# Edge-attention scores with two halves' tiles together, one ring of six PSUM banks, and a written order on three engines

## The chip, the core and the metric

The kernel runs on one core of a Trainium2 chip. A core has TensorE (PE: matrix products and transposes, written into PSUM banks of 128 x 512 float32), VectorE (DVE), ScalarE (ACT), GpSimd (POOL) and SyncE (SP, which only issues DMAs). Each engine works through its own instructions in the order in which they were laid down, and waits on semaphores for the others. The metric is the device time of one execution in microseconds (us). In the profile, PEld is the loading of weights into TensorE, which overlaps PE, and SPq, ACTq and POOLq are the engines' instruction queues where they issue DMAs.

## The reference, cut to what matters

Four graph layers follow each other on x, 128 graphs of 64 nodes with 256 features. Each adds its output to x and normalises. The change lies in the third (layer 2), an attention over 512 edges with 4 heads of 64 features:

```python
Xq = (H @ W_lin.T).reshape(bt, n, h, dh)
Xv = (H @ W_val.T).reshape(bt, n, h, dh)
Qs = Xq[:, src]
Kt = Xq[:, dst]
e = jnp.einsum('behd,hd->beh', jax.nn.leaky_relu(Qs + Kt, 0.2), a)
e = e + jnp.log(A0[src, dst] + EPS)[None, :, None]
e_t = e.transpose(1, 0, 2)
m = jax.ops.segment_max(e_t, src, num_segments=n)
ex = jnp.exp(e_t - m[src])
attn = ex / jax.ops.segment_sum(ex, src, num_segments=n)[src]
Vt = Xv[:, dst].transpose(1, 0, 2, 3)
Y = jax.ops.segment_sum(attn[..., None] * Vt, src, num_segments=n)
return Y.transpose(1, 0, 2, 3).reshape(bt, n, d) @ W_out.T
...
x = _layernorm(x + layer(x))          # after each of the four layers
```

## The kernel before

**Data.** X lies in SBUF as 64 tiles of 128 rows (two graphs each) by 256 features. `NT` is 64, `NQ` and `HU` are 16. Layer 0 and most of layer 1 come first and are not touched.

**The last pass of layer 1** (`last_pass`) finishes layer 1 for two tiles at a time: `normed` scales them on ACT (L2039), PE transposes them (L2048), DVE adds them to X (`ln.add`: the join, L1350), takes statistics (L1353, L1354), and `flush` gets a factor by a chain of small instructions between DVE and ACT (`inv_sqrt`, L1272 to L1278, then L1365) and scales X on ACT (L1369). It is a generator that is driven beside the first 16 steps of layer 2.

**Scores** (`scores`) goes through 32 steps k of two tiles.
- `transposed(k)` transposes X on PE (L2136) and copies it to xT on DVE (L2138), two steps ahead.
- `maps(k + 1, xT)` multiplies xT by both weight matrices on PE (L2148). The query half w is split in a high part xh, copied on ACT into the reduced float32 type that the PE multiplies faster (L2153), and a remainder xl, a subtraction on DVE (L2154). The value half xv is copied on ACT (L2165) and sent to DRAM by SP (L2166).
- `edges(c)`, for each feature half c, multiplies xl and xh by a 0/1 matrix of the edges (L2188), which gives Q[src] + K[dst] of 512 edges for 128 features in one bank. ACT copies the bank to SBUF as xs (L2194), DVE makes the leaky relu in place (L2195): 4 tiles a half, 8 a step.
- `products` multiplies xs by the vector a (the table az) into score banks sc (L2124): 8 matmuls a half, each into 32 rows.

The order of a step is: edges of half 0, maps, edges of half 1, then both halves' products; in the first 16 steps the last pass stands between these and the products are issued a half at a time. Beyond that a scheduler settles the order of each engine; `after` makes the products of a cluster wait together.

**PSUM.** The stage uses eight banks: `pp` has two (tag "m": transposes, maps, mixing, W_out), `pg` two pairs (tag "l": edge tiles), `pc` two (tag "sc": scores).

**Softmax and values.** After 16 steps the scores of half of the graphs are complete. `softmax` adds log A, subtracts the segment maximum by two scans (DVE: L2231, L2235, L2236), exponentiates (ACT), transposes and sums by matmuls, and scatters the result to DRAM by indirect DMAs on POOL (L2275); `fetch` reads it back as a table M on SP and POOL (L2285). Then `values` runs beside the last scoring steps and beside layer 3: `mapped` loads xv back as xr on POOL's queue (L2300), `load` copies a piece mc of the table on ACT (L2292), `mixed` multiplies on PE (L2312) and copies yT on ACT (L2315), and W_out (L2335) is followed by `ln.add`, which flushes every four tiles.

**Layer 3** starts as values go on; its POOL addition is L2404.

The driver reads, cut:

```python
run(*beside * 4)                    # last_pass alone
run(*[sc_] * (NQ - 1))              # scoring steps, last_pass inside
soft += [softmax(h) for h in range(2)]
run(*[sc_] * (HU - NQ + 1))
run(*[sc_, soft[0]] * 6)
fetch(0)
run(*[sc_] * 3)
constants()
run(*[sc_, val] * 7)
```

Of the kernel before, what the change touches and what calls it, by code (L numbers as in the profile page):

```python
# [8 lines left out]
F32 = mybir.dt.float32  # L9
# [7 lines left out]
N = 64  # L17
NB = 128
D = 256
# [1317 lines left out]
class Norm:  # L1337
# [6 lines left out]
    def add(self, t, src, n=1, dve=0):  # L1344

        nc = self.nc
        if not self.todo:
            self.mv = self.pool.tile([P, self.n, 2], F32, tag="ln_mv", name="ln_mv")
        x = self.X[:, t : t + n, :].rearrange("p n d -> p (n d)")
        nc.vector.tensor_tensor(x, src, x, ALU.add)  # L1350
        for k in range(t, t + n):
            st = self.pool.tile([P, 6], F32, tag="ln_st", name="ln_st")
            nc.vector.bn_stats(st, self.X[:, k, :])  # L1353
            nc.vector.bn_aggr(self.mv[:, len(self.todo), :], st)  # L1354
            self.todo.append(k)
        if len(self.todo) == self.n:
            self.flush(dve)

    def flush(self, dve=0):
        nc, n = self.nc, len(self.todo)  # L1360
        rs = self.pool.tile([P, self.n], F32, tag="ln_rs", name="ln_rs")
        inv_sqrt(nc, self.pool, rs[:, :n], self.mv[:, :n, 1], 1e-5)
        if self.act:
            sh = self.pool.tile([P, self.n], F32, tag="ln_sh", name="ln_sh")
            nc.vector.scalar_tensor_tensor(sh[:, :n], self.mv[:, :n, 0], -1.0, rs[:, :n], ALU.mult, ALU.mult)  # L1365
        for k, t in enumerate(self.todo):
            x = self.X[:, t, :]
            if self.act and k < n - dve:
                nc.scalar.activation(x, x, AF.Identity, bias=sh[:, k : k + 1], scale=rs[:, k : k + 1])  # L1369
                continue  # L1370
            nc.vector.tensor_scalar(x, x, self.mv[:, k, 0:1], rs[:, k : k + 1], ALU.subtract, ALU.mult)
        self.todo = []


@with_exitstack
def tile_adj_resnorm(ctx: ExitStack, tc: tile.TileContext, I: dict, out: bass.AP, layers: int = 4):
# [655 lines left out]
    def last_pass():  # L2032

        ln = Norm(nc, sy, X, 8, act=True)

        def normed(h):
            y = sy.tile([P, 2, 2 * P], F32, tag="y", name="y")
            for c in range(2):
                s.activation(y[:, c, :], Y[h // 2][:, c, h % 2 * 2 * P : (h % 2 + 1) * 2 * P], AF.Identity,  # L2039
                             bias=sh2[:, c : c + 1], scale=sc2[:, c : c + 1])  # L2040
            return y

        y = normed(0)
        for h in range(2 * NQ):
            ps = pp.tile([P, 512], F32, tag="m", name="m")
            for i in range(2):
                for c in range(2):
                    te.transpose(ps[:, i * D + c * P : i * D + (c + 1) * P], y[:, c, i * P : (i + 1) * P], ident)  # L2048
            with in_order(v, h < 3):
                ln.add(2 * h, ps, 2)  # L2050
            if h == 1:
                keep_awake(pg.tile([P, 2, 512], F32, tag="l", name="l")[:, 0, :], 2)
            yield
            with in_order(s, h < 5):
                if h < 2 * NQ - 1:
                    y = normed(h + 1)
            with in_order(s, h < 5), in_order(v, h < 3):
                if h < 3 or h % 2 == 0 or h == 2 * NQ - 1:
                    ln.flush()
            yield  # L2060
# [10 lines left out]
    with ExitStack() as l2:  # L2071
# [3 lines left out]
        pp = own1(l2, name="l2p", bufs=2, space=PSUM)  # L2075
        sx = own1(scoring, name="l2x", bufs=2, side="right")
        pg = own1(scoring, name="l2g", bufs=2, space=PSUM)
# [17 lines left out]
        for c in range(2):  # L2095
            for h in range(2):
                o = (h + 1) * HU - 1
                v.tensor_tensor(az[:, c, o : o + 1], heads[:, h : h + 1], acol[:, c : c + 1], ALU.mult)
# [5 lines left out]
        taken, drawn, last = {}, {}, []  # L2104
        beside = [iter(())]
        soft = []

        def after(ins, those, how=mybir.DependencyClass.Sync):
            for i in those:
                tc.add_manual_dep(ins.ins, i.ins.name, mybir.DependencyInfo(how, mybir.DependencyReason.DATA),  # L2110
                                  reason="together")

        def products(todo, held):

            xss = [held.pop(x) for x in todo]
            mms = []
            for (k, c), (xs, _) in zip(todo, xss):
                half, u_ = divmod(k, HU)
                if u_ == 0:
                    sc[half][c] = pc.tile([P, 512], F32, tag="sc", name="sc")  # L2120
                for b in range(2):
                    for i in range(2):
                        q = 32 * (2 * b + i)
                        mms.append(te.matmul(sc[half][c][q : q + 32, :], az[:, c, HU - 1 - u_ : 3 * HU - 1 - u_],  # L2124
                                             xs[b, i], start=(u_ == 0), stop=(u_ == HU - 1)))
                if u_ == HU - 1:
                    run(*[soft[half]] * (2 if half and not c else 1))
            after(mms[0], [x for _, ready in xss for x in ready])
            after(mms[0], last[-1:], mybir.DependencyClass.NoSync)

        def transposed(k):

            ps = pp.tile([P, 512], F32, tag="m", name="m")
            for i in range(2):
                for c in range(2):
                    te.transpose(ps[:, i * D + c * P : i * D + (c + 1) * P], X[:, 2 * k + i, c * P : (c + 1) * P], ident)  # L2136
            xT = sx.tile([P, 2, 2, P], F32, tag="xT", name="xT", bufs=1)
            v.tensor_copy(xT.rearrange("p i c n -> p (i c n)"), ps)  # L2138
            return xT

        def maps(k, xT, apart=False):

            xq, xv = [], sx.tile([P, 2, D], F32, tag="xv", name="xv")
            pss = [pp.tile([P, 512], F32, tag="m", name="m") for _ in range(2)]

            def product(i, cols):
                for c in range(2):
                    te.matmul(pss[i][:, cols], xT[:, i, c, :], wqv[:, c, cols], start=(c == 0), stop=(c == 1))  # L2148

            def first(i):  # L2150
                hi = sx.tile([P, D], F32R, tag="xh", name="xh", bufs=4)
                lo = sx.tile([P, D], F32R, tag="xl", name="xl", bufs=4)
                drawn[i] = s.copy(hi, pss[i][:, :D])  # L2153
                v.tensor_tensor(lo, pss[i][:, :D], hi.bitcast(F32), ALU.subtract)  # L2154
                xq.append((lo, hi))
# [5 lines left out]
            for i in range(2):  # L2161
# [3 lines left out]
                s.copy(xv[:, i, :], pss[i][:, D:])  # L2165
            nc.sync.dma_start(xvd[k], xv)  # L2166
            return xq

        def scores():
# [4 lines left out]
            xq = maps(0, xT, True)  # L2174
            next(beside[0])
            next(beside[0])
            xT = transposed(1)


            held = {}  # L2180

            def edges(c):
                xs, ready = {}, []
                for i in range(2):
                    pl = pg.tile([P, 2, 512], F32, tag="l", name="l")
                    for part, b in ((0, 0), (0, 1), (1, 0), (1, 1)):
                        r = slice(b * N, (b + 1) * N)
                        mm = te.matmul(pl[:, b, :], xq[i][part][r, c * P : (c + 1) * P], GGr[r, :],  # L2188
                                       start=(part == 0), stop=(part == 1))
                        if not b and not part:  # L2190
                            after(mm, taken.pop(i, []) + ([drawn[i]] if c == 0 else []))
                    for b in range(2):
                        x = xs[b, i] = sx.tile([P, E], F32, tag="xs", name="xs", bufs=10)
                        taken.setdefault(i, []).append(s.copy(x, pl[:, b, :]))  # L2194
                        ready.append(v.scalar_tensor_tensor(x, x, 0.2, x, ALU.mult, ALU.max))  # L2195
                held[k, c] = xs, ready
                last.append(mm)

            for k in range(K):
                apart, xn = k < NQ, None  # L2200
                edges(0)
                if apart:
                    run(*beside)
                    if k:
                        products([(k - 1, 1)], held)
                if k < K - 1:
                    xn = maps(k + 1, xT)
                if apart:
                    run(*beside)
                elif k < K - 2:  # L2210
                    xT = transposed(k + 2)
                edges(1)
                xq = xn
                if apart:
                    run(*beside)
                    products([(k, 0)], held)
                    xT = transposed(k + 2)
                    run(*beside)
                else:
                    products([(k - 1, 1), (k, 0)], held)  # L2220
                if k == K - 1:
                    products([(k, 1)], held)
# [75 lines left out]
        def mapped(k):  # L2298
            x = sm.tile([P, 2, D], F32, tag="xr", name="xr", bufs=3)
            nc.gpsimd.dma_start(x, xvd[k])  # L2300
# [44 lines left out]
        sc_, beside[0] = scores(), last_pass()  # L2345
        run(*beside * 4)
        run(*[sc_] * (NQ - 1))
        keep1.close()
        beside[0] = iter(())
# [33 lines left out]

# [130 lines left out]
```

## Time and profile before

| | us |
|---|---|
| median of 3 runs | 2222.89 |
| lowest and highest | 2221.97, 2224.12 |
| profiled execution | 2226.54 |
| its span, from first to last instruction | 2224.8 |

The granted TensorE clock, averaged over the span, is 0.994 of full speed. The stages that the change touches lie in these parts of the span:

| us from the span's start | what runs |
|---|---|
| up to 1673 | layer 0, layer 1 |
| 1673 to 1699.26 | start of layer 2 with the last pass of layer 1 |
| 1699.26 to 1839.41 | 13 scoring steps with the last pass beside them |
| 1839.41 to 1958.18 | 12 scoring steps, softmax and table fetch of the first half |
| 1958.18 to 2005.63 | 4 scoring steps with values |
| 2005.63 to 2026.70 | the end of scoring |
| 2026.70 to 2224.8 | remaining values, layer 3 |

In the profile's lines, "L2148" is a line of the kernel, "m<-wqv,xT" the output tile and the input tiles, "128x512" partitions by elements, and "x8" the number of instructions put together. "[3.62 <-ACT xv L2165]" says that the engine had been idle for 3.62 us before, and what it had waited for.

### The profile page before, as it was taken

Reading aid. Unit: us, or ns where it says so; the run is one execution under the profiler, and the core shown is the slowest. Engines: PE = TensorE matmul, PEld = TensorE weight load, DVE = VectorE, ACT = ScalarE, POOL = GpSimd, SP = SyncE. Lnnn points to the kernel's source line nnn. Section 1 sums busy time; section 2 is a strip of 40 time slices with the busy share of each in tenths; the row PEclk is TensorE's granted clock in tenths of the full one; section 3 lists DMA queues with packets and bytes.
Section 4 is the critical chain, followed back from the end, with each engine's and each line's share of the span. In section 5 each row is a group of like instructions: output and inputs, shape, how many; then the busy total and the mean of one; then the engine's idle time right before and its main releaser. Section 6 shows DMA issues by size and latency. Waiting matters only on the chain. (4 is left out here: it accounts for less than half of the span.)

```text
span 2224.8 us, 30044 instructions
## 1 busy us (share of the span) xinstructions
PE 2169.1 (97%) x8816; PEld 1212.6 (55%) x8816; DVE 1831.2 (82%) x9347; ACT 940.3 (42%) x1729; POOL 162.9 (7%) x196
## 2 busy tenths in 40 slices
PE   8999999999999999999999999999999999999997
PEld 6545665445665445665444654554434443446887
DVE  5788887888898899889899899787968888766788
ACT  1432322433322333332333222334437886667675
POOL 0111111101000000000000000000000000101532
PEclk9999999999999999999999999999999999999999
DMA  7000010111010111010111000012210010411522
GB/s 236 22 20 38 1 39 1 38 38 57 1 39 1 39 38 57 1 39 1 38 39 57 1 20 19 1 74 95 76 58 20 29 42 29 108 50 42 159 84 80
DMA packets 44668, 101.56 MB, mean 46 GB/s; under 512 B 5296, under 2 KB 23856, under 8 KB 43216
## 3 DMA queue, kind: packets, MB, share of 16 engines
q1 hardware_dynamic: 38384, 84.64, 11.0%
q0 software_dynamic: 3984, 14.40, 2.3%
q8 instruction: 70, 1.15, 0.2%
q10 hardware_dynamic: 2128, 0.54, 0.1%
q14 instruction: 102, 0.84, 0.1%
HBM read 67.97 MB, written 31.59 MB: 45 GB/s over the span
## 5 line engine op out<-in xcount | busy, mean ns | idle before, releaser
L1740 PE MATMUL pq<-H,wi 128*128 128x512 f32 (+1 forms) x1952 | 780.6, 540 | 1.5 <-ACT gate L1780 1.3
L1780 ACT ACTIVATE gate<-pq,bl 128x512 f32<-128x512 f32 (+1 forms) x504 | 315.8, 632 | 614.3 <-PE pq L1756 500.5
L1740 PEld LDWEIGHTS pq<-H,wi 128*128 128x128 f32 x1952 | 365.5, 190 | 336.8 <-issue 270.0
L1756 PE MATMUL pq<-lh,wh 128*128 128x512 f32 (+1 forms) x1152 | 461.3, 528 | 0.9 <-DVE lh L1798 0.8
L1756 PEld LDWEIGHTS pq<-lh,wh 128*128 128x128 f32 x1152 | 218.4, 190 | 202.5 <-issue 143.5
L1783 ACT ACTIVATE gate<-lc 128x512 f32<-128x512 f32 (+1 forms) x144 | 83.6, 581 | 278.8 <-DVE lc L1795 103.2
L2195 DVE SCALAR_TENSOR_TENSOR xs<-xs 128x512 f32<-128x512 f32 x256 | 165.3, 679 | 18.2 <-ACT xs L2194 15.1
L2194 ACT COPY xs<-l 128x512 f32<-128x512 f32 x256 | 135.6, 597 | 36.5 <-PE l L2188 30.4
L2148 PE MATMUL m<-wqv,xT 128*128 128x512 f32 (+1 forms) x264 | 123.1, 599 | 2.9 <-DVE xT L2138 1.3
L2012 PE MATMUL ps<-h,w 128*128 128x512 f32 x256 | 114.5, 604 | 5.0 <-ACT h L2006 2.7
L1369 ACT ACTIVATE X<-X,ln_sh,ln_rs 128x256 f32<-128x256 f32 x187 | 97.5, 594 | 37.1 <-DVE ln_sh L1365 21.2
L1958 PE MATMUL ps<-at,w 128*128 128x512 f32 x256 | 113.1, 593 | 0.0
L803 POOL PARTITION_ALL_REDUCE qQ<-qSG x62 | 74.0, 1193 | 508.5 <-DVE pc L135 268.9
L2012 PEld LDWEIGHTS ps<-h,w 128*128 128x128 f32 x256 | 48.3, 192 | 65.1 <-issue 55.1
L2148 PEld LDWEIGHTS m<-wqv,xT 128*128 128x128 f32 x264 | 46.0, 189 | 65.3 <-issue 39.8
L1958 PEld LDWEIGHTS ps<-at,w 128*128 128x128 f32 x256 | 47.2, 190 | 52.8 <-issue 51.4
L1353 DVE BATCH_NORM_STATS2 ln_st<-X 128x6 f32<-128x256 f32 x192 | 73.9, 415 | 1.2
L2124 PE MATMUL sc<-xs,az 128*32 128x512 f32 x512 | 74.5, 612 | 0.1
L131 DVE SCALAR_TENSOR_TENSOR CS<-GA,qE 64x1 f32<-64x1 f32 x294 | 61.8, 210 | 9.5
L1798 DVE TENSOR_TENSOR lh<-gate 128x512 f32<-128x512 f32 (+1 forms) x72 | 43.1, 602 | 31.5 <-ACT gate L1780 31.5
L131 DVE SCALAR_TENSOR_TENSOR GA<-qtg,CS,GA 64x1 f32<-64x1 f32 x294 | 61.6, 209 | 8.4
L1959 DVE BATCH_NORM_STATS2 st<-ps 128x6 f32<-128x512 f32 x64 | 43.8, 684 | 26.9 <-PE ps L1958 26.9
(637 smaller groups left out, 3452.0 us busy)
## 6 DMA issues: line engine op xcount, KB each, us to landing
wi<-in_WihT_dram SPq DMA_DIRECT2D x16, 1024.0 KB, 4.8
wh<-in_WhhT_dram SPq DMA_DIRECT2D x12, 1024.0 KB, 6.1
xd<-X SPq DMA_DIRECT2D x16, 512.0 KB, 2.6
X<-xd SPq DMA_DIRECT2D x16, 512.0 KB, 3.4
xv<-xv SPq DMA_DIRECT2D x32, 256.0 KB, 2.0
xr<-xv POOLq DMA_DIRECT2D x32, 256.0 KB, 3.0
X<-in_x_dram SPq DMA_DIRECT2D x15, 512.0 KB, 8.9
out_dram<-X SPq DMA_DIRECT2D x15, 512.0 KB, 2.9
```

Of the source, the lines that this page charges most:

```text
L131: self.nc.vector.scalar_tensor_tensor(o, a, s, b, op0, op1)
L1369: nc.scalar.activation(x, x, AF.Identity, bias=sh[:, k : k + 1], scale=rs[:, k : k + 1])
L1740: te.matmul(ps, wi[:, kk, o * P : (o + 1) * P], at(kk, k), start=(kk == 0), stop=(k == 0 and kk == 1))
L1756: te.matmul(ahead[gt, c], wh[:, kk, o * P : (o + 1) * P], hst[:, kk, :M], start=False, stop=(kk == 1))
L1780: s.activation(gates[gt][:, c, :M], ps, AF.Tanh if gt == 2 else AF.Sigmoid, bias=bl[:, p - 1, o : o + 1])
L1783: s.activation(*due.pop())
L1958: te.matmul(ps, w1[:, k, c * P : (c + 1) * P], at[:, k, :], start=(k == 0), stop=(k == 1))
L2012: te.matmul(ys[c], w2[:, k, c * P : (c + 1) * P], h[:, k, :], start=(k == 2), stop=(k == 1))
L2124: mms.append(te.matmul(sc[half][c][q : q + 32, :], az[:, c, HU - 1 - u_ : 3 * HU - 1 - u_], xs[b, i], start=(u_ == 0), stop=(u_ == HU - 1)))
L2148: te.matmul(pss[i][:, cols], xT[:, i, c, :], wqv[:, c, cols], start=(c == 0), stop=(c == 1))
L2194: taken.setdefault(i, []).append(s.copy(x, pl[:, b, :]))
L2195: ready.append(v.scalar_tensor_tensor(x, x, 0.2, x, ALU.mult, ALU.max))
```

## The change

1. In step k the edge tiles of half 1 of step k - 1 and of half 0 of step k are computed together (16 matmuls), then come maps(k + 1), the transposes for step k + 2, the transposes of the last pass (`turned`, up to two), and the 16 products.
2. The leaky relu is written as 0.8 relu(z) + 0.2 z. relu(z) is taken straight from PSUM, on ACT for b = 0 and on DVE for b = 1, in the place of ACT's copy and DVE's leaky relu; the factor 0.8 goes into az.
3. The linear part 0.2 z needs only a . w for each node: ACT copies w whole to SBUF, POOL multiplies it by a (`arow`), DVE sums over features (one reduce a step, issued a step later), and `linear` adds it to the scores with one matmul for each half of the graphs and each c.
4. `pp` is one ring of six single banks for all but the scores. After scoring a pool of two banks takes its place.
5. `follow` makes an instruction of scoring stand behind the one recorded last on its engine (PE, ACT, DVE).
6. The last pass is divided in `turned`, `prepare`, `whole`, `closed`; `Norm.add` in `join`, `stats`, `root`, `flush`. Scales of X (L1369) are issued two at a time between the maps.
7. The xv writes of steps 23 to 26 and the xr loads of steps 15 to 18 are issued by ACT.

The diff, cut:

```diff
+    def root(self, dve=0):
...
+        return [lambda a=(k, t): scaled(*a) for k, t in enumerate(todo)]
...
+        def turned(h):
+            ps, x = pp.tile([P, 512], F32, tag="m", name="m"), y.pop(h)
+...
+            ln.join(2 * h, ps, 2)
...
-        pp = own1(l2, name="l2p", bufs=2, space=PSUM)
+        pp = own1(scoring, name="l2p", bufs=6, space=PSUM)
-        pg = own1(scoring, name="l2g", bufs=2, space=PSUM)
...
+        arow = sx.tile([P, D], F32, tag="arow", name="arow", bufs=1)
+...
+        v.memset(linb, 0.0)
...
+        def follow(make, *a, eng=te, **k):
+            turn = next(i for i in reversed(nc.cur_bb.bb.instructions) if i.engine == eng.engine)
+            ins = make(*a, **k)
+            tc.add_manual_dep(ins.ins, turn.name, ...)
+            return ins
+
+        def linear(half, c):
+            for b in range(2):
+                r = slice(b * N, (b + 1) * N)
+                v.tensor_scalar(linb[r, c, b], lin[r, half, c], 0.2, None, ALU.mult)
+            follow(te.matmul, sc[half][c], linb[:, c].rearrange("p b i h u -> p (b i h u)"), GG, start=False, stop=False)
...
         def maps(k, xT, apart=False):
...
-                drawn[i] = s.copy(hi, pss[i][:, :D])
-                v.tensor_tensor(lo, pss[i][:, :D], hi.bitcast(F32), ALU.subtract)
+                follow(s.copy, hi, x, eng=s)
+                follow(s.copy, w, x, eng=s)
+                follow(v.tensor_tensor, lo, w, hi.bitcast(F32), ALU.subtract, eng=v)
...
-                s.copy(xv[:, i, :], pss[i][:, D:])
-            nc.sync.dma_start(xvd[k], xv)
+                follow(s.copy, xv[:, i, :], pss[i][:, D:], eng=s)
+                nc.gpsimd.tensor_tensor(whole[:, i, :], whole[:, i, :], arow, ALU.mult)
+                yield
+            sums.append(lambda: follow(v.tensor_reduce, lin[...], whole..., AX.X, ALU.add, eng=v))
+            (s if 22 < k < 27 else nc.sync).dma_start(xvd[k], xv)
...
-                    pl = pg.tile([P, 2, 512], F32, tag="l", name="l")
+                    pl = [pp.tile([P, 512], F32, tag="m", name="m") for _ in range(2)]
...
-                        x = xs[b, i] = sx.tile([P, E], F32, tag="xs", name="xs", bufs=10)
-                        taken.setdefault(i, []).append(s.copy(x, pl[:, b, :]))
-                        ready.append(v.scalar_tensor_tensor(x, x, 0.2, x, ALU.mult, ALU.max))
+                        x = xs[b, i] = sx.tile([P, E], F32, tag="xs", name="xs", bufs=8)
+                        ready.append(follow(v.tensor_scalar, x, pl[b], 0.0, None, ALU.max, eng=v) if b
+                                     else follow(s.activation, x, pl[b], AF.Relu, eng=s))
...
             for k in range(K):
+                ha, hb = (h if h < 2 * NQ else None for h in (2 * k + 3, 2 * k + 4))
+                if k:
+                    edges(k - 1, 1, xl)
+                edges(k, 0, xq)
+                if hb:
+                    prepare(hb)
+                if last:
+                    closed(last)
+                steps = maps(k + 1, xT) if k < K - 1 else iter((None,) * 3)
+                next(steps)
+                while sums:
+                    sums.pop()()
+                scales(2)
+                next(steps)
+                scales(2)
+                xl, xq = xq, next(steps)
+                if k < K - 2:
+                    xT = transposed(k + 2)
+                if ha:
+                    with in_order(v, True), in_order(te, True):
+                        turned(ha)
+                        if hb:
+                            turned(hb)
+                        ln.stats(2 * ha, 2)
+                products([(k - 1, 1), (k, 0)] if k else [(k, 0)], held)
+                if hb:
+                    prepare(hb + 1)
...
-            nc.gpsimd.dma_start(x, xvd[k])
+            (s if 14 < k < 19 else nc.gpsimd).dma_start(x, xvd[k])
...
         scoring.close()
+        pp = own1(l2, name="l2m", bufs=2, space=PSUM)
```

## The prediction

> **What bounds the kernel now.** The page's first part says TensorE: busy 97% of a 2224.8 us span, VectorE 82%, ScalarE 42%. That is an average over four layers, and the change touches 1673 to 2027 us only, so the next view is the busy time by windows. Columns: window, length, then busy time and count of each engine, granted clock, DMA share, GB/s.
>
> ```profile
> PE 2169.1 (97%) x8816; PEld 1212.6 (55%) x8816; DVE 1831.2 (82%) x9347; ACT 940.3 (42%) x1729; POOL 162.9 (7%) x196
> 1699.26:1839.41 140.15, 139.31 (x679) 57.13 (x677) 122.66 (x353) 119.76 (x272) 1.82 (x3) 1.00 0.10 34
> 1839.41:1958.18 118.77, 110.84 (x600) 49.51 (x596) 90.93 (x167) 74.41 (x159) 11.45 (x13) 0.97 0.24 67
> 1958.18:2005.63 47.45, 45.34 (x336) 23.58 (x336) 32.01 (x67) 32.89 (x68) 2.29 (x5) 1.00 0.15 51
> 2005.63:2026.70 21.07, 19.58 (x154) 9.39 (x152) 16.67 (x37) 15.84 (x32) 1.08 (x2) 1.00 0.12 39
> ```
>
> The windows are cut where a step's maps start: 13 steps with the last pass of layer 1 between them (10.78 us each), 12 with softmax and table fetch, 4 with values, the tail. PE is busy 99% of the first, so only less PE work shortens it; but DVE (88%) and ACT (85%) are close behind. PE's timeline then tells how well it is used. First a half step of the first stage, then a later step.
>
> ```profile
> 1774.45 1.98 PE L2148 MATMUL m<-wqv,xT 128*128 128x512 f32 x4
> 1779.80 1.05 PE L2124 MATMUL sc<-xs,az 128*32 128x512 f32 x2
> 1780.77 0.65 PE L2048 MATMUL m<-ident,y 128*128 128x128 f32 x4
> 1781.36 1.06 PE L2124 MATMUL sc<-xs,az 128*32 128x512 f32 x6
> ...
> 1881.26 0.66 PE L2136 MATMUL m<-ident,X 128*128 128x128 f32 x4
> 1882.98 1.92 PE L2124 MATMUL sc<-xs,az 128*32 128x512 f32 x16
> 1884.83 0.50 PE L2188 MATMUL l<-edge_s,xl 64*128 64x512 f32 x2
> 1885.94 3.70 PE L2148 MATMUL m<-wqv,xT 128*128 128x512 f32 x8
> ```
>
> A cluster of products cut in two by transposes costs 1.05 for its 2 and 1.06 for its 6, while 8 uncut took 1.06 (1773.45): the cut costs about 1 us. Sixteen together take 1.92. The second and third L2148 and L2188 rows between (left out) have the maps cut too, four and four. Last the one long stall, on PE's timeline (three rows) and ACT's (one); in brackets the idle time before and who ended it:
>
> ```profile
> 1949.30 1.12 PE L2136 MATMUL m<-ident,X 128*128 128x128 f32 x4 [3.62 <-ACT xv L2165]
> 1952.35 3.20 PE L2124 MATMUL sc<-xs,az 128*32 128x512 f32 x16
> 1955.48 0.50 PE L2188 MATMUL l<-edge_s,xl 64*128 64x512 f32 x2
> 1948.88 0.37 ACT L2165 COPY xv<-m 128x256 f32<-128x256 f32 x1 [4.45 <-DMA xv<-xv]
> ```
>
> The xv transfers stood on SP behind the table fetch of 1927.20; ACT waited for a buffer, PE for ACT, and then 3.57 us of work took 6.18: after a gap of 3.62 us PE ran slow (clock 0.59 in 1950 to 1956) and lost 2.6 more. A gap of 1.31 us (2099.28) cost nothing further.
>
> **PE's step after.** Edges: 8 matmuls took 1.13 (1771.74 to 1772.87), with the first pair 0.34, later ones 0.235 and the last 0.33; so 16 together 2.08. Maps undivided 3.57 (two halves 1.92 each before). Four transposes 0.58. Sixteen products 1.85. Sum 8.08, and 9.25 with two sets of transposes of `turned`: 1.53 below 10.78.
>
> **What may be longer: DVE and ACT.** Relu now reads PSUM and frees the bank; half goes to ACT (copy L2194, 0.51 us between starts), half to DVE (as join L1350, 0.61). Eight leaky relus and eight copies become four and four. Added are ACT's copy of w (2 x 0.25), DVE's reduce (1 a step; rows of 128x128 and 64x64 took 0.288 and 0.211, so 0.75 for 512 columns, between 0.3 and 1.0) and 64 POOL multiplies (L2404 has them at 0.73). POOL has 8 us from whole w to its sum a step later, against 1.5 of work: hidden; if the six indirect DMAs (1.27 each) stood in front it would be 7.6 + 1.5 = 9.1, one step late by 1. `follow` also writes down the order of PE, ACT and DVE, so each waits in its own queue. The built order gives the round of a first-stage step: four relus 4 x 0.61 = 2.44; statistics 1.00 (L1353 at 1675.27 to L1272 at 1676.27); L1272 to the first scale L1369 1.43 (1676.27 to 1677.70); two scales on ACT 1.00 (to 1678.70); two copies 0.25 + 0.37; 0.05 of hand-over; second difference L2154 0.34; xT 0.61 (1679.32 to 1679.93); two joins 1.22; statistics of the other half 1.00. Sum 9.71, above PE's 9.25. I take 9.7; ends 9.25 (ACT's part overlapped) and 10.5 (relu from PSUM at 0.80 instead of 0.61).
>
> **The sum, stage by stage** (profiled execution: 2224.8 span, 1.74 around it, 2226.54 in all, 3.65 above the median 2222.89; differences apply to both).
>
> - Start to 1699.26: 0 (-1 to +3). The memset of `linb` and the copy of `arow` stand before the first join, step 0 is shorter.
> - 13 steps: 13 x (9.7 - 10.78) = -14.0 (-19.9 to -3.6). The split product (1 us every second step) and divided maps go.
> - 1839.41 to 1958.18: 12 x 8.08 = 97.0, and PE work as in the trace of before: softmax transposes 1.03, sums 1.89, shares 1.7, constants 0.74, mixing 0.9, one `turned` 0.58, two linear matmuls 2.0 (as a broken product cluster, 1 each): 8.84. Stalls, where `follow` puts softmax work in a queue ahead of relus and PE waits for banks: score addition 0.69 and scan 1.22 on DVE, less 0.6 that I let the ring carry, 1.3 twice; reciprocals 0.9, shares 0.75, constants 0.3; eT on ACT 0.5; together 5.05. Two mc copies on ACT (2.11 at 1955.26) less 0.26 that the table's landing hides, 1.85. Total 112.7: -6.0. In it lies the gain of the xv transfers of four steps on ACT's queue: the 3.62 and the 2.6 go. Those issues stand behind the copy they need, hence cost ACT only the issue.
> - Four value steps: 4 x (8.08 + mixing 0.9 + a wait for mc of 0.2, as at 1956.45 + wo 1.92) = 44.4. `ln.add` stands in DVE's queue in front of the relus: 1.0 in each step without flush. With one (every second) ACT's queue holds the whole of it ahead of relu: counted from the end of wo, join at 0.11 (1980.72 to 1980.83), statistics 0.72 on, L1272 another 1.00 on (1.84), the first scale 1.43 on (3.27), four scales 2.00, relu 0.68: bank free at 5.95. The six banks take three pairs of edge matmuls, 0.5 each, so the fourth pair wants it at 1.5: 4.4 of stall, then 2.6 of slow clock. 2 x 1.0 + 2 x 7.0 = 16.0. Total 60.4: **+13.0**. Before, scales and evictions stood mixed, and PE waited nowhere over 0.41.
> - Tail: the last half's edges now come after the products, and their relu (0.68, 0.1 of hand-over) has nothing beside it: +0.8. Layer 3: xr loads of four steps on ACT's queue, PSUM pool of two banks made again: 0 (-2.3 to +1).
>
> Sum 0 - 14.0 - 6.0 + 13.0 + 0.8 = -6.2: 2216.7 by the median, 2220.3 profiled.
>
> The slow clock is the part with a rule against it. The trace: gap 3.62, loss 2.6; gap 1.31, none. The Trainium skill, "TensorE: Matmul & The Clock Gate", section "Part 1: The HAM clock gate", says that the array falls to half clock after an idle window of about 3.4 us and needs as long a busy one to come back. By its figures the loss is 3.4 x 0.5 = 1.7 a time, an estimate, and the sum -8.0. A row speaks against its window: after a gap of 2.19 (1664.72) eight matmuls took 5.40 that take 3.70 at full clock. So shortening a gap to 2.2 need not save the loss, and I keep 2.6.
>
> **Rivals.**
> *Stalls hide better (faster).* ACT and DVE buffers (eight xs) and the ring may carry a part of the 22.9 us of stalls priced above (5.05 + 1.85 + 16.0). For it: before, PE waited under 0.41 in value steps. Against: the order is now fixed. Half hidden is -11.5: 2205; all, 2194.
> *The fixed round is the bound (slower).* PE fills 99% because a scheduler had laid DVE's and ACT's work where it fitted. In a written order each passage between engines shows: L1272 to L1274 took 0.20 (1676.27 to 1676.47), and five more such per step make 9.7 into 10.7. Price 13 us per us of round: 2216.7 + 13 = 2230; it decides from 10.18 on (no gain), from 10.5 it is slower by more than 0.2%. For it: DVE's 88% and ACT's 85%; DVE still has to do four relus, two joins, four statistics, two differences, xT and a sum, and each waits for ACT or PE. Against: DVE's own busy sum falls by four leaky relus less a reduce.
> *No difference.* A round of 10.0 to 10.4: within 0.2% (4.45 us, about what a measurement can tell): 2222.
> That the change does not do what it says can be left out: the built order shows clusters of sixteen and undivided maps.
>
> **How the numbers follow.** Forecast 0.40, about 2208 to 2221 (of it 0.32 below 2218.4, 0.08 within 0.2%); stalls hidden 0.22; no difference 0.10; slower 0.28. Faster 0.32 + 0.22 = 0.54, same 0.08 + 0.10 = 0.18, slower 0.28. The range runs from 2199 (three quarters of the stalls hidden, 17.2) to 2236 (a round of 11.2); 0.08 lie below, 0.12 above.
>
> **What would show it.** Right: first-stage steps of 9.7, no L2124 row of 2 or 6, relus of 0.68, POOL multiplies of 0.73 with no wait for them, no ACT wait for an xv transfer; in value steps two gaps of over 4 us before edges, released by ACT's relu, with a granted clock under 1 after. Wrong: steps above 10.5 with PE waiting for DVE in every one; or no gap above 2 us in the value steps; or a slower layer 3.

## The result and the profile after

The changed kernel is slower by a little: 2227.89 us median (2226.60 to 2231.32, 18 runs) against 2223.14 for the kernel before (2220.14 to 2228.92, 18 runs); ratio 1.0021, 95% interval 1.0014 to 1.0028. That is 4.75 us. Measured again beside the experiments it was 1.0018 (1.0009 to 1.0027). The two profiled executions, 2228.17 and 2226.54, differ by only 1.6, since that of before was 3.4 above its median; the other 3 us are differences between executions that no stage below can be charged with.

The page's first part for the changed kernel: PE has 13 us less to do in all, and DVE 50.

```profile
PE 2156.3 (97%) x8828; PEld 1227.0 (55%) x8828; DVE 1781.5 (80%) x9261; ACT 891.8 (40%) x1663; POOL 206.3 (9%) x256
```

Busy time by windows, cut at the same places as before (the maps of the same steps), plus two windows that the prediction did not cut: from the last scoring maps to the first matmul of layer 3, and from there to the last matmul. Columns: window, length, busy time and count of PE, PEld, DVE, ACT, POOL, clock, DMA share, GB/s.

```profile
1673.00:1702.23 29.23, 22.66 (x98) 13.16 (x96) 18.19 (x57) 15.84 (x38) 2.91 (x4) 0.88 0.05 19
1702.23:1826.25 124.02, 122.57 (x677) 61.58 (x677) 108.16 (x314) 104.16 (x248) 20.83 (x29) 1.00 0.10 33
1826.25:1944.69 118.44, 111.22 (x613) 54.08 (x613) 72.30 (x140) 57.44 (x138) 28.23 (x37) 0.97 0.26 75
1944.69:2001.03 56.34, 47.86 (x339) 25.71 (x337) 26.56 (x64) 28.21 (x63) 8.11 (x12) 0.92 0.11 38
2001.03:2042.09 41.06, 37.53 (x358) 23.72 (x356) 27.96 (x69) 24.19 (x47) 4.70 (x8) 0.98 0.15 46
2042.09:2213.41 171.32, 162.38 (x1609) 146.13 (x1608) 122.48 (x421) 110.88 (x234) 62.10 (x90) 0.97 0.34 93
```

The last two windows of the kernel before, for the comparison:

```profile
2005.63:2049.34 43.71, 38.80 (x355) 24.73 (x353) 31.62 (x82) 32.59 (x61) 3.23 (x6) 0.96 0.14 43
2049.34:2212.01 162.67, 159.29 (x1610) 143.84 (x1609) 126.57 (x421) 110.09 (x234) 64.58 (x94) 1.00 0.34 98
```

| stretch | before | after | measured | predicted |
|---|---|---|---|---|
| 1673 to the maps of step 1 | 26.26 | 29.23 | +3.0 | 0 |
| 13 steps with layer 1's last pass | 140.15 | 124.02 | -16.1 | -14.0 |
| 12 steps with softmax and table | 118.77 | 118.44 | -0.3 | -6.0 |
| 4 steps with values | 47.45 | 56.34 | +8.9 | +13.0 |
| to the first matmul of layer 3 | 43.71 | 41.06 | -2.7 | +0.8 |
| layer 3 with the other values | 162.67 | 171.32 | +8.7 | 0 |

At its first matmul of layer 3 the changed kernel is 7.2 us ahead (2042.09 against 2049.34), where the stages ahead of it were predicted at -6.2 together; that the two lie so close is in part luck, since the misses in the single stages (+3.0, -2.1, +5.7, -4.1, -3.5) nearly cancel. Layer 3, whose code is not changed but for the xr loads, gives it all back and 1.4 more. PE's timeline there, and ACT's and POOL's:

```profile
2082.01 0.98 PE L2390 MATMUL m<-mc,xr 64*64 64x64 f32 x32
2088.06 3.78 PE L2413 MATMUL ps<-wo,yT 128*128 128x256 f32 x8 [5.07 <-ACT ag L2481]
2094.65 1.22 PE L2390 MATMUL m<-mc,xr 64*64 64x64 f32 x32 [2.81 <-ACT yT L2393]
2095.80 3.38 PE L2413 MATMUL ps<-wo,yT 128*128 128x256 f32 x8
```
```profile
2074.07 0.33 ACTq L2378 DMA_DIRECT2D xr<-xv  x1
2086.38 1.05 ACT L2370 COPY mc<-M 128x512 f32<-128x512 f32 x1 [11.95 <-DMA M<-attn_d]
```
```profile
2062.01 0.74 POOL L2483 TENSOR_TENSOR X<-X,cb 128x256 f32<-128x256 f32 x1
2069.01 2.14 POOL L2363 DMA_DIRECT2D M<-attn_d  x4 [6.26 <-issue]
```

ACT waits 11.95 us for the second half's table, with its next piece mc (step 16) at the head of the queue, and everything else that PE needs from ACT (ag, which is layer 3's own copy at L2481, the scales, yT) stands behind it. PE is idle 5.07 and 2.81, and runs slow between and after: W_out took 3.78 and 3.38 instead of 1.99. In the kernel before, the same copy was issued at 2098.18, behind yT of step 15 (2092.63), and PE's two waits at this place were 1.01 and 1.31. PE's and ACT's timelines of the kernel before:

```profile
2093.30 1.99 PE L2335 MATMUL ps<-wo,yT 128*128 128x256 f32 x8 [1.01 <-ACT yT L2315]
2099.28 0.92 PE L2312 MATMUL m<-mc,xr 64*64 64x64 f32 x30 [1.31 <-ACT mc L2292]
```
```profile
2098.18 2.04 ACT L2292 COPY mc<-M 128x512 f32<-128x512 f32 x2
```

In the changed kernel it stands some twenty ACT instructions earlier, right behind yT of step 14 (2073.77) and in front of ag. Also visible: POOL issues its half of the table 6.26 us after its last addition, long after SP's half (2060.46).

### The profile page after: what moved, and what is told of

It reads as the page before. It is cut to its first block, busy times and chain, and to the rows that moved or that the text cites. A ratio compares the mean times of both kernels' runs of the same rounds, so it can differ in the third digit from the quotient of the medians.

```text
span 2226.4 us, 30062 instructions
## 1 busy us (share of the span) xinstructions
PE 2156.3 (97%) x8828; PEld 1227.0 (55%) x8828; DVE 1781.5 (80%) x9261; ACT 891.8 (40%) x1663; POOL 206.3 (9%) x256
## 5 line engine op out<-in xcount | busy, mean ns | idle before, releaser
L2148 DVE TENSOR_SCALAR xs<-m 128x512 f32<-128x512 f32 x128 | 79.6, 677 | 18.5 <-PE m L2148 18.5
L2148 PEld LDWEIGHTS m<-wqv,xT 128*128 128x128 f32 x264 | 51.1, 204 | 66.4 <-issue 49.6
L2148 ACT ACTIVATE xs<-m 128x512 f32<-128x512 f32 x128 | 68.7, 598 | 44.3 <-PE m L2148 43.5
L2219 POOL TENSOR_TENSOR xq<-xq,arow 128x256 f32<-128x256 f32 x64 | 46.8, 732 | 377.3 <-DVE xl L2148 377.2
L2148 PE MATMUL m<-edge_s,xl 64*128 64x512 f32 x256 | 68.4, 449 | 13.3 <-ACT xs L2148 11.8
L2148 DVE TENSOR_TENSOR xl<-xq,xh 128x256 fp32r<-128x256 f32 x64 | 27.3, 426 | 56.6 <-ACT xq L2148 56.6
```

Source lines behind the costliest of these rows:

```text
L2148: ins = make(*a, **k)
L2219: nc.gpsimd.tensor_tensor(whole[:, i, :], whole[:, i, :], arow, ALU.mult)
```

## Experiments

**Who owns the loss in layer 3.** `load` keeps mc of steps 16 and 17 in program order, which orders it behind the one ACT instruction recorded just ahead of it; this is called its pin here. Before, that was the last scale or layer 3's work on ACT. Since the xr load of step 17 moved to ACT, the instruction just ahead is this DMA, which itself is ordered behind nothing. Theory A: so mc(16) lost its place. Rivals: B, the table is late whoever waits; C, the loads cost something on ACT's queue; D, the wait matters only for the 7 us lead.

Loads back on POOL:

```diff
-            (s if 14 < k < 19 else nc.gpsimd).dma_start(x, xvd[k])
+            nc.gpsimd.dma_start(x, xvd[k])
```

> The changed kernel with the xr loads of steps 15 to 18 back on POOL's queue; nothing else. Theory A (the lost pin): the copy mc of step 16 is ordered only behind the ACT instruction recorded just before it; since xr(17) moved to ACT that is a DMA which itself is ordered behind nothing, so mc(16) slid some ten instructions up ACT's queue and holds it 11.95 us for the second table. Then this undo puts mc(16) back behind yT of step 15, the two PE gaps of 5.07 and 2.81 go, and the time falls by 7 to 9 us, to 2219 to 2221, below the kernel before. Theory B (the table is late whoever waits, since its POOL half was issued 6.26 us late behind SP's half): the gaps stay, the time stays at 2226 to 2229.

Measured: 2223.29 (2226.12 for before beside it), ratio 0.9986 (0.9977 to 0.9995); set against the 1.0018 to 1.0021 of the changed kernel, some 7 to 8 us gained. The 5.07 and 2.81 are gone, yet a new wait came, so the layer takes 166.67 from its first matmul to its last (2044.71 to 2211.38) and not 162:

```profile
2088.20 1.61 PE L2390 MATMUL m<-mc,xr 64*64 64x64 f32 x32 [3.50 <-DMA xr<-xv]
```

On POOL's queue the loads stand behind the table's issues (2071.88) and layer 3's additions. B is refuted: POOL's half of the table was issued as late (6.40 idle before it), and PE did not wait for the table.

Loads on ACT, in program order:

```diff
-            (s if 14 < k < 19 else nc.gpsimd).dma_start(x, xvd[k])
+            if 14 < k < 19:
+                tc.keep_in_program_order(s.dma_start(x, xvd[k]))
+            else:
+                nc.gpsimd.dma_start(x, xvd[k])
```

> The changed kernel with the xr loads of steps 15 to 18 still issued by ACT, but each kept in program order on it. Theory A (lost pin): mc(16) is again behind the work recorded before it, the same gain as with the loads on POOL, 2219 to 2221. Theory C (what costs is the ACT queue's part in the loads itself: their issue, or 1.05 MB more on that ring beside the table): no gain, 2226 to 2229.

Measured: 2217.59, ratio 0.9962 (0.9948 to 0.9975), more than expected. Layer 3 takes 160.32 (2042.49 to 2202.81), 11.0 less than in the changed kernel and 2.35 less than before: that is the 1.01 and 1.31 that PE had waited there before. C is refuted.

Only the recording order of two lines:

```diff
-                    if k < K - 2:
-                        xr.append(mapped(k + 2))
                     mn = load(k + 1) if k < K - 1 else None
+                    if k < K - 2:
+                        xr.append(mapped(k + 2))
```

> The changed kernel with two lines of values exchanged: mc of the next step is recorded before the xr load instead of after it. The xr loads stay on ACT and stay free in the order; only what stands ahead of mc(16) in the recording is the last scale again, not a DMA. Theory A (lost pin): mc(16) is behind yT of step 15, the gaps of 5.07 and 2.81 go, first basis to last matmul takes 160 to 163 us instead of 171.3, and the ratio to before is 0.996 to 0.998. Theory C (the loads on ACT's queue, or a later start of them, is what counts): no gain, 1.001 to 1.003.

Measured: 2219.26 (2223.33), ratio 0.9979 (0.9970 to 0.9988); layer 3 161.26 (2042.96 to 2204.22). PE's and ACT's timelines, mc(16) and mc(17) after the scales, and one gap of 1.31 left:

```profile
2091.50 0.97 PE L2390 MATMUL m<-mc,xr 64*64 64x64 f32 x32 [1.31 <-ACT mc L2370]
```
```profile
2088.41 2.08 ACT L1383 ACTIVATE X<-X,ln_sh,ln_rs 128x256 f32<-128x256 f32 x4 [2.02 <-DVE ln_mv L1363]
2090.40 2.04 ACT L2370 COPY mc<-M 128x512 f32<-128x512 f32 x2
```

The xr loads are as free as in the changed kernel, so what counts is what stands ahead of mc in the recording: A.

This part alone in the kernel before:

```diff
-            nc.gpsimd.dma_start(x, xvd[k])
+            (s if 14 < k < 19 else nc.gpsimd).dma_start(x, xvd[k])
```

> The kernel before, with this one part of the change alone: xr loads of steps 15 to 18 issued by ACT. Theory A: mc(16) slides up here too, ACT is blocked from about 2083 until the table lands (about 2089.5), the work behind it is late, and the kernel is slower than before by 3 to 8 us (2226 to 2231). Theory D (the wait matters only because the changed kernel comes 7 us sooner to this place): within 1.5 us of before.

Measured: 2236.73 (2226.12), ratio 1.0049 (1.0036 to 1.0063): 10.6 slower, more than A's 3 to 8, because the table landed at 2093.8 and not at the 2089.5 that I assumed. D is refuted.

```profile
2095.50 3.71 PE L2335 MATMUL ps<-wo,yT 128*128 128x256 f32 x8 [8.03 <-ACT ag L2402]
```
```profile
2093.82 1.05 ACT L2292 COPY mc<-M 128x512 f32<-128x512 f32 x1 [11.94 <-DMA M<-attn_d]
```

**The value steps.** Two gaps as predicted, in steps 28 and 30 of the changed kernel, PE's timeline:

```profile
1970.88 0.79 PE L2148 MATMUL m<-edge_s,xl 64*128 64x512 f32 x2 [4.24 <-ACT xs L2148]
1972.03 5.53 PE L2148 MATMUL m<-wqv,xT 128*128 128x512 f32 x8
...
1999.88 0.79 PE L2148 MATMUL m<-edge_s,xl 64*128 64x512 f32 x2 [4.24 <-ACT xs L2148]
2001.03 4.69 PE L2148 MATMUL m<-wqv,xT 128*128 128x512 f32 x8
```

The test takes statistics, root and scales out of the way of the relus:

```diff
-                    ln.add(2 * (k - 1), po, 2)
+                    if k < 6:
+                        ln.join(2 * (k - 1), po, 2)
+                        joined.append(2 * (k - 1))
+                    else:
+                        ln.add(2 * (k - 1), po, 2)
...
+                if joined:              # in scores, behind both edges(...)
+                    with in_order(v, True):
+                        ln.stats(joined.pop(), 2)
+                    if len(ln.todo) == ln.n:
+                        closed(None)
```

> The changed kernel, but the statistics, the inverse root and the scales of X of the value steps are recorded in the next scoring step behind its edges (as those of layer 1's last pass are), scales two at a time between the maps; the join stays where it was. My step for the value stage (relu queued behind the flush: two gaps of 4.24 us, then maps of 5.53 and 4.69 instead of 3.70) gives 8.5 + 2.4 + 1.6 = 12.5 less; so 11 to 13 us faster than the changed kernel if nothing takes it back, 2215 to 2217. Rival (the second table's arrival sets the end of this stretch anyway): 0 to 3 us faster, the gain turned into a longer wait of ACT for the table.

Measured: 2217.59 (2226.12), ratio 0.9953 (0.9940 to 0.9967). No gap remains in these four steps, and they take 43.81 (maps at 1946.62 and 1990.43) instead of 56.34: 12.5 less, and the two gaps are the cause of 8.5 of it. That it is the very number expected is in part luck: 1.1 of the slow maps that the expectation counted lie behind this stretch, and the two steps without a flush got some 0.5 shorter each, which it did not count. The wait for the table got longer by 1.4 (6.20 and 3.08), since the pin is still lost, and layer 3 by 2.7. By the ratios the whole is some 15 us below the changed kernel (the interval alone is 3 wide either way), in the profiled execution, the slowest of five, 6.9; only the gain in the four steps is read off directly.

**The first stage.** Is its step of 9.48 the round through DVE and ACT? Two tests. Left out: the linear part.

```diff
-                nc.gpsimd.tensor_tensor(whole[:, i, :], whole[:, i, :], arow, ALU.mult)
...
-            sums.append(lambda: follow(v.tensor_reduce, ...))
```

> The changed kernel without the linear part of the leaky relu (no multiplication on POOL, no reduce on DVE; the sum added to the scores is zero, so the scores lack 0.2 z). In the trace the reduce (0.68) is followed by 0.76 us in which DVE waits for ACT's copy of w. If the first-stage step of 9.48 is the written round through DVE and ACT, as my sum had it, the wait only grows to 1.4 and the step stays 9.4 to 9.5. If DVE's amount of work is the bound, the step falls to PE's 9.25.

Measured: the maps start at 1731.30, 1740.78, 1750.26, 1759.76: 9.48 a step, and DVE waits 1.35. (One run, 2236.64, 9.6 above before; its wait for the table was 9.84 with 2.81 behind it, and other waits in the softmax stage had changed too; these are not explained, and only the step is used.) DVE's timelines, changed kernel first, then this one:

```profile
1782.51 0.68 DVE L2148 TENSOR_REDUCE lin<-xq 128x8 f32<-128x512 f32 x1
1783.94 0.42 DVE L2148 TENSOR_TENSOR xl<-xq,xh 128x256 fp32r<-128x256 f32 x1 [0.76 <-ACT xq L2148]
```
```profile
1783.84 0.42 DVE L2148 TENSOR_TENSOR xl<-xq,xh 128x256 fp32r<-128x256 f32 x1 [1.35 <-ACT xq L2148]
```

Taken out of the round: the two scales.

```diff
-                scales(2)
                 next(steps)
-                scales(2)
+                scales(4)
```

> The changed kernel with all four scales of X behind the second half of the maps instead of two and two. The two scales (1.00) then no longer stand in the round between the first scale and the second difference. If the round is the bound, it shrinks below PE's sum and the first-stage step falls from 9.48 to 9.25, 13 steps x 0.23 = 3 us less up to 1826; if PE and the six banks give the 9.48, nothing changes.

Measured: the maps start every 9.00 us (1741.82, 1750.82, 1759.82), 0.48 less and below my 9.25 for PE: PE's own sum was 0.25 too high, since three sets of four transposes take 1.40 together (1781.36 to 1782.76 here) and not 3 x 0.58, while the edges take 2.20 (1775.62 to 1777.82) and not 2.08. In the changed kernel the same maps start at 1740.93, 1750.40 and 1759.88; PE's timeline here:

```profile
1750.82 3.70 PE L2148 MATMUL m<-wqv,xT 128*128 128x512 f32 x8
1759.82 3.70 PE L2148 MATMUL m<-wqv,xT 128*128 128x512 f32 x8
```

The step was the round; at 9.00 PE has become the bound (busy for all of the 81.01 us from 1741.82 to 1822.83). One run, 2225.02 beside 2227.02 for before.

**Two losses that I had not listed.** The final flush of layer 1's last pass ends in front of the edges of step 15: a gap of 3.31 that ends with ACT's relu, then maps (1838.36) of 5.40 instead of 3.70:

```profile
1837.69 0.50 PE L2148 MATMUL m<-edge_s,xl 64*128 64x512 f32 x2 [3.31 <-ACT xs L2148]
```

With its two scales on DVE:

```diff
-                    closed(None)
-                    scales(2)
+                    closed(None, 2)         # root(dve=2)
+                    with in_order(v, True):
+                        scales(2)
```

> The changed kernel with the last two scales of layer 1's last pass on DVE instead of ACT. In the trace the gap of 3.31 us before edges at 1837.69 ends with ACT's relu, which stands behind two scales that end at 1837.07; then the eight maps take 5.40 instead of 3.70. My reading (ACT's queue): ACT's relus start 2 us sooner, the gap shrinks to 1.0 to 1.6 and the slow maps go: 3 to 4 us less up to the next step. Rival (DVE is what is late there): the gap stays at about 3, since DVE's relus start 0.7 later.

```profile
1837.00 0.99 PE L2148 MATMUL m<-edge_s,xl 64*128 64x512 f32 x2 [1.21 <-ACT xs L2148]
1838.75 3.70 PE L2148 MATMUL m<-wqv,xT 128*128 128x512 f32 x8 [0.54 <-DVE xs L2148]
```

The gap is 1.21, with 0.54 for DVE's relus behind it, and the maps take 3.70. Up to the next step's maps 2.6 us are gained (1849.25, against 1851.72 in the repeat of the changed kernel, which had started 0.15 earlier), less than the 3 to 4 expected. By its one run (2229.22) no gain shows; it ends in the same wait for the table, 4.84 and 2.80.

At the start, `whole(2)` has its flush in DVE's queue ahead of xT(1):

```diff
-            whole(2)
             xT = transposed(1)
+            whole(2)
```

> The changed kernel with transposed(1) recorded ahead of whole(2), so that the copy xT of step 1 is not behind the flush of tiles 4 and 5 in DVE's queue. The trace has a gap of 2.25 us before the maps at 1692.04 and then 5.40 instead of 3.70 for them. If the queue is the cause, the gap goes below 0.5 and the maps take 3.70: 3 to 4 us less at the following map start. If the scale of tiles 2 and 3 itself is late, nothing changes.

```profile
1689.08 3.70 PE L2148 MATMUL m<-wqv,xT 128*128 128x512 f32 x8
1699.81 3.70 PE L2148 MATMUL m<-wqv,xT 128*128 128x512 f32 x8 [0.72 <-DVE xs L2148]
```

The gap of 2.25 ahead of the first of these maps is gone and they take 3.70. But part of the wait moved on to relus and edges of the next step, and at step 14 only 1.6 are left (1824.23 with a first X transpose at 1678.71, against 1826.25 and 1679.17). The time of the one run (2230.64) shows nothing.

**All together.** First the loads kept in order, the late flush of values, the last flush on DVE and the changed start:

> The changed kernel as it is, to stand beside the others on one chip: 0.14 to 0.28% above the kernel before (ratio 1.0021), as in its own measurement.

> All of it: xr loads of ACT kept in program order, the value steps' flush behind the edges, the last flush of layer 1 on DVE, transposed(1) ahead of whole(2). If the four losses are separate they add up: 11 (basis to the last matmul 160.3 instead of 171.3) + 12.5 + 3.5 + 3.5 = 30 less than the changed kernel, ratio to before 0.988 to 0.990. If the second table's arrival is the floor behind them, a wait of ACT for it comes back in layer 3 and 8 to 12 of the 30 are lost: 0.991 to 0.995.

Measured in one session: changed kernel 2228.55, ratio 1.0018; the four repairs 2203.19, ratio 0.9902 (0.9887 to 0.9917), 25 us less where 30 were expected. The start and the last flush had given 1.6 and 2.6 alone, and not 3.5 each; and in this profile the eight maps behind the last flush took 5.17 again, though the gaps ahead of them were only 1.20 and 0.54. PE has no gap in layer 3 until the end, so the table's arrival is no floor. With the scales behind the maps as well:

> All four repairs together (they measured 0.990 of before) and the scales behind the maps. If the round bounds the first stage: 3 us less again, 0.9885 to 0.9895. If not: 0.990 to 0.991.

Measured: 2194.57 (2227.02 beside it), ratio 0.9852 (0.9835 to 0.9868). This beats both kernels, by more than expected. In the profiles the first matmul of layer 3 comes 6.7 us sooner than in the kernel of four repairs (2022.13 against 2028.80), as 13 x 0.48 = 6.2 asks; my 3 us had PE's floor at 9.25. The two ratios lie further apart than that (0.0050, some 11 us); they are from two sessions, each against its own runs of before, and their intervals come within 0.0019 of each other, some 4 us, so that the difference can be the 6.7 of the profiles.

## Why the prediction was wrong

**The step that failed: "Layer 3: xr loads of four steps on ACT's queue ... 0 (-2.3 to +1)".** I costed the loads as issues and asked only what they would stand in front of. What mattered was that another instruction's place was defined by "behind the one recorded before". The built order has mc(16) right after the xr load and in front of ag; I read the order of scoring and not that of layer 3. The prediction named a slower layer 3 among its signs of being wrong, without a cause or a price. Layer 3 measured +8.7 in the profile, and 10.1 and 11.0 came back when the place was restored in two ways (161.26 and 160.32 of 171.32). Without it the changed kernel is at 0.9962 to 0.9979, that is 4.7 to 8.4 us below before; the sum without that step said -6.2.

**The start, predicted 0, measured +3.0.** PE waits 1.69, 2.22 and 2.25 there, and maps(1) took 5.40; the upper end that I gave was +3. With transposed(1) ahead of whole(2), 1.6 to 2 came back.

**First stage, predicted -14.0, measured -16.1.** The mechanism held: a round through relu, statistics, root, scales, second difference, joins; 9.48 instead of 9.71, because the statistics of the second half took 0.87 and not 1.00 and the relus 2.37. The slower rival (hand-overs not overlapped, 10.7) is refuted.

**Softmax stage, predicted -6.0, measured -0.3.** I listed stalls by DVE's long work and missed the biggest: the final flush of the last pass (3.31 and 1.7 of slow clock) in front of step 15's relus. The stalls that I did list at 5.05 were too high: a gap of 0.76 behind the scan and edges stretched over their usual 2.20 come to some 2.7. The table's wait was 2.99, and the edges behind it took 3.43, together 4.2 where I had 1.85. By these rows the stage's miss of 5.7 is made up, all but 0.1, of 5.0 for the flush, -2.4, +2.4, and 0.6 for twelve steps of 8.13 instead of 8.08.

**Value stage, predicted +13.0, measured +8.9.** The stall was 4.24 twice (4.4 predicted), the slow clock 2.3 and 1.5 (2.6 predicted; edges 0.45 over their usual 0.70, maps 5.37 and 4.62 to the next start instead of 3.54; the second maps lie behind the end of the stretch), and the steps without flush lost some 0.4 to 0.6, not 1.0. The wait that I gave as the longest of these steps before, 0.41, was not: a row at 1962.47 has 0.59. **Tail, +0.8 predicted, -2.7 measured**: I priced one wait behind the last edges; PE waits 1.61, 1.20 and 0.68 for DVE there. Against that, the softmax transposes and sums behind it run without the 0.72, 1.32 and 1.38 that PE waited before, and W_out at their end takes 1.99 (2038.19) where it took 3.62 (2043.81). No run tests these apart.

**The rule that was weighed.** The Trainium skill, "TensorE: Matmul & The Clock Gate", "Part 1: The HAM clock gate", says an idle window of about 3.4 us halves the clock. The estimate of 1.7 a gap that the prediction worked out from it lies between the 1.5 and 2.3 measured for gaps of 4.24. The page also says that the window runs freely, so that it depends where in it the work falls. That would fit a pair of rows: the same gap of 2.25 at the same place was followed by eight maps in 5.40 in the changed kernel (granted clock 0.57 from 1692 to 1695) and in 3.70 in the kernel with the loads on POOL (1.00 from 1692.8 to 1695). That gaps of 2.25 do it at all does not agree with its 3.4, and still less do the 1.20 and 0.54 in the kernel of four repairs, behind which the clock was 0.50 from 1838 to 1840.

```profile
1692.04 5.40 PE L2148 MATMUL m<-wqv,xT 128*128 128x512 f32 x8 [2.25 <-DVE xT L2148]
```
```profile
1693.03 3.70 PE L2148 MATMUL m<-wqv,xT 128*128 128x512 f32 x8 [2.25 <-DVE xT L2148]
```

**Left open.** Why POOL's half of the table is issued 6.3 us late; SP's half is in flight just then, and the last scatter may land late for it, but no run here changes that order. And the 3 us between the medians' difference and the profiles'.

## What to carry to other kernels

When an instruction is moved to another engine, look for rules that speak of "the instruction before" on that engine: a DMA issue there that is ready early takes the pin from whatever comes next, and the cost shows where that next instruction waits, here 60 us after the last scoring step. Read the built order of every stretch that holds a moved instruction, not only of the loop under study. And where an order is written by hand, look for the one chain that stands in a queue ahead of work that frees a buffer: two scales in the wrong place were 0.48 us a step, a flush ahead of relus 6 us a time.

## What the runs showed of the hardware that was not expected

The same gap of 2.25 us ahead of maps(1) was followed by slow matmuls in seven executions and not in two others (5.40 or 3.70 for eight), so single profiles differ by 1.7 us for each such place though the program is the same up to there. Shorter gaps are not safe either: 1.20 and 0.54 in the place of the last flush were followed by eight maps in 5.17 in the kernel of four repairs, and 1.21 and 0.54 in 3.70 with the last flush's repair alone. And transposes in a row take a little less: a set of four took 0.54 to the next start where one `turned` stood alone (1830.22), two sets 0.97 (1725.94).
